# A two-layer cross-attention kernel: the image outputs of the last four heads on GpSimd, the image softmax behind the normalization, one Gram group a step earlier

## The chip, the cores and the metric

One core of a Trainium2 chip runs the kernel. The metric is the device time of one launch in microseconds (us), the median of several runs. The profile is of one execution, with times in us from the start of its span. Engines: PE (matrix multiply; PEld its weight loads), DVE (VectorE), ACT (ScalarE), POOL (GpSimd), SP (the queue that issues the DMAs).

## The reference

Two cross-attention layers, one after the other, over 64 sequences of 256 rows and 320 channels (20 heads of 16), each with its own context of 77 rows of 512 channels. All is float32. Layer 0 is plain attention. Layer 1 adds an image branch:

```
q = heads(x @ W_q);  k_t, v_t from the first 73 context rows;  k_ip, v_ip from the last 4
probs_t  = softmax(q k_t / 4);            text_out = probs_t v_t
qsem     = l2norm(probs_t @ text_ehs);    sem = qsem @ l2norm(ip_ehs)
probs_ip = softmax(q k_ip / 4 + 0.5 sem) * spatial_mask          # 4 tokens per head
out      = (text_out + probs_ip v_ip) @ W_out + b_out + x
```

(Layer 0 has 77 context rows as text, and an image branch is formed only in layer 1.) The change concerns the product `probs_ip v_ip`, for heads 16 to 19, and when the softmax of `probs_ip` is computed.

## The kernel before

**Steps.** Two sequences (b = 0, 1) make a pair p, 32 pairs in all. The attention of a pair in one layer is cut into ten units: for each b, five units u of 128 rows by 8 heads (the fifth holds the last four heads of both row halves). The main loop runs over steps g; p = g // 10 and k = g % 10 name a step ("step 7" is k = 7). Step g computes the scores of layer 0 for unit g, the scores of layer 1 for unit g - 13, and the products with the Gram matrix and the values ("semantics", L755 and L761) of layer 1 for unit g - 15. All three go into one PSUM tile `sc`, which takes four banks and exists once. So the first semantics of a step (L755) can't start until ACT has copied `sums` (L1064) out of the `sc` of the step before, and that copy waits for DVE to have read `sc` for the last time (L772, L775). The start of the first L755 is used below as the start of a step.

**What each engine does in a step, in order.** PE: semantics, scores (L641), the transposes of layer 1's probabilities (L705, L706), a first group of fillers, the transposes of layer 0's probabilities (again L705, L706), a second group of fillers, and after units 1 and 4 the products with the values (`pv`, L788, L793). DVE: what is in `early`, draining a projection (L601) in steps 0 and 2, row maxima and differences of both layers (L659, L661), the products with the Gram result (L772, L775), layer 0's row sums and their reciprocals (L687, L688), what is in `later`, and a last reduction (L1136). ACT: copies of the transposes (L712 layer 1, L731 or L720 layer 0), the exponential of layer 0 (L669), `sums` (L1064), the exponentials of layer 1 (L672, L673), copies for the fillers. POOL: a small copy (L676), the normalization of layer 0's probabilities (L692), and many small products that place values, keys and Gram matrices in block form.

**Fillers.** `fillers(k, p)` is a table written by hand: which keys, queries, values, Gram matrices and projections are made in which step, for pairs p + 1 to p - 3. `add(0, ...)` is the first group, `add(1, ...)` the second, `add(2, ...)` the third, after the second. Each takes one of two PSUM tiles `ms` (pool `pms`) in turn; transposes take one of two tiles `tr` (pool `ptr`) in turn. In 6 of the pairs 2 to 30 (3, 8, 13, 18, 23, 28) steps 6 and 8 hold two groups of `value_rows` (L379), otherwise one.

**The image branch of layer 1.** Five units after its first, a sequence is through (`ends`, in step 4 or 9). Then, by steps: `image_scores` (L882 on DVE, L883 and L884 on POOL) is put in `later` of the next step (5 or 0); `image_shifted` (`most`, L889 on DVE; L890 on POOL) and `image_exponential` (`num`, L893 on ACT) in `early` of the step after (6 or 1); `image_weights` (L900, L901 on DVE; L902, L850 on POOL) in `early` of the third (7 or 2). `later` runs ahead of the normalization, `early` at the head of a step. In step 7 `image_transposed` (L914, `itr`) transposes the weights of both sequences, all 80 columns (20 heads of 4 tokens); in step 8 `image_attend` multiplies heads 0 to 15 with the block-diagonal image values (L926), and `image_attend_last` heads 16 to 19 (L947, 80 rows), which DVE adds to `last` (L951). The block values `vip` are loaded by 20 DMAs per sequence (L475).

**The text branch.** `text_output` (step 4 or 9) divides by the row sums on POOL (L850, `an`); `text_transposed` (steps 5 and 0) transposes two blocks of 128 channels per row half (L837) and the last 64 channels (L838), and ACT copies both (L840, L841) to `main` and `last`, which `project` of layer 1 reads in step 9.

**Order.** `keep_order` fixes the order as written on PE, ACT, DVE and POOL. An instruction that waits holds up all that follow on its engine. The order of SP's DMAs after the first steps is chosen by the framework's scheduler.

## Time and profile before

| | us |
|---|---|
| median of 3 runs (lowest, highest) | 2617.92 (2614.57, 2618.2) |
| profiled execution, device time | 2612.19 |
| its span, first to last instruction | 2610.4 |
| one pair in the middle, ten steps | 77.44 |

The profiled execution is 5.7 us below the median. Its granted TensorE clock is 0.998 over the span. The steps are very regular: the starts of the first L755 of each step, read from the timeline over the whole trace, give these lengths, as medians over the pairs 3 to 30:

| step | 0 | 1 | 2 | 3 | 4 | 5 | 6 | 7 | 8 | 9 |
|---|---|---|---|---|---|---|---|---|---|---|
| us | 8.08 | 9.39 | 8.61 | 7.45 | 8.68 | 6.42 | 6.95 | 6.96 | 7.09 | 7.81 |

In the six pairs with two groups of `value_rows`, step 6 takes 9.10 and step 8 takes 9.24. A line of the timeline view gives start, duration, engine, line, operation, what is written from what, the count of merged instructions, and in brackets the engine's idle time before it with what ended it.

### The profile page before, as it was taken

The numbers are of one execution on the slowest core, as the hardware profiler recorded it, in microseconds if no ns is written. First come the engines' busy times: TensorE is split into PE (matmuls) and PEld (weight loads), VectorE is DVE, ScalarE is ACT, GpSimd is POOL, SyncE is SP. The second block draws the span as 40 slices with busy tenths as digits, with TensorE's granted clock in tenths as the row PEclk, the third lists the DMA queues.
The fourth block names the chain that finished last, engine by engine and source line by source line (L and its number), as shares of the span: only waits on it lengthen the run. The fifth ranks groups of instructions, "written<-read, shape, count | busy, mean of one in ns | idle before, by whom it ended". The sixth has DMA issues, their size and how long they took to land.

```text
span 2610.4 us, 74097 instructions
## 1 busy us (share of the span) xinstructions
PE 2552.0 (98%) x27026; PEld 1979.1 (76%) x27026; DVE 1971.3 (76%) x3641; ACT 1535.6 (59%) x3989; POOL 1439.9 (55%) x3514
## 2 busy tenths in 40 slices
PE   7999999999999999999999999999999999999998
PEld 5677777777777777777777777777777777777677
DVE  4577777777787777787777787777777778777864
ACT  3465665665665665665665665665665566666553
POOL 2456555566555556555556555556555565555542
PEclk9999999999999999999999999999999999999999
DMA  5212211112111112111112111112111112111100
GB/s 164 72 29 58 58 43 48 43 51 55 52 51 38 51 51 55 55 48 39 51 52 55 51 52 43 47 52 56 52 51 39 51 53 55 47 50 34 29 22 23
DMA packets 154658, 132.28 MB, mean 51 GB/s; under 512 B 48248, under 2 KB 132984, under 8 KB 154296
## 3 DMA queue, kind: packets, MB, share of 16 engines
q1 hardware_dynamic: 153432, 126.38, 18.0%
q8 instruction: 217, 3.56, 0.6%
q14 instruction: 145, 1.19, 0.2%
q10 hardware_dynamic: 864, 1.15, 0.1%
HBM read 89.53 MB, written 33.91 MB: 47 GB/s over the span
## 4 chain that ended last, share of the span: by engine, by line
PE 84%; DVE 7%; DMA 3%; ACT 2%; POOL 1%; issue 1%; SPq 1%; DVEq 0%; POOLq 0%; ACTq 0%
PE sc L755 12%; PE tr L705 11%; PE o_ps L528 8%; PE sc L641 7%; PE v_ps L379 6%; PE sc L761 4%; PE q_ps L528 4%; PE q_ps L555 4%; PE k_ps L334 3%; PE o_ps L616 3%; DVE w L661 3%; PE pv L788 2%; PE o_ps L537 2%; DVE mx L659 2%; PE q_ps L557 2%; PE rtr L706 2%
## 5 line engine op out<-in xcount | busy, mean ns | idle before, releaser
L659 DVE TENSOR_REDUCE mx<-sc 128x8 f32<-128x584 f32 (+1 forms) x640 | 497.3, 777 | 446.9 <-PE sc L641 446.8
L692 POOL TENSOR_TENSOR parts<-w,sm 128x512 f32<-128x512 f32 (+1 forms) x640 | 439.5, 707 | 301.9 <-ACT parts L673 177.8
L661 DVE TENSOR_TENSOR w<-sc,mx 128x616 f32<-128x616 f32 x640 | 511.8, 800 | 67.0 <-ACT w L669 0.5
L712 ACT COPY pt<-tr 128x512 f32<-128x512 f32 x320 | 186.8, 584 | 431.9 <-PE tr L705 427.5
L705 PE MATMUL tr<-ident,parts 128*128 128x128 f32 x2560 | 409.6, 283 | 12.5 <-POOL parts L692 5.2
L755 PEld LDWEIGHTS sc<-gv,pt 64*128 64x128 f32 x5120 | 316.9, 187 | 96.0 <-ACT sums L1064 47.3
L705 PEld LDWEIGHTS tr<-ident,parts 128*128 128x128 f32 x2560 | 282.5, 141 | 123.4 <-issue 88.0
L755 PE MATMUL sc<-gv,pt 64*128 64x94 f32 x5120 | 356.3, 278 | 17.4 <-ACT sums L1064 17.2
L676 POOL COPY att<-w 128x32 f32<-128x32 f32 x320 | 66.8, 209 | 469.7 <-DVE w L661 469.2
L669 ACT ACTIVATE w<-w 128x616 f32<-128x616 f32 x320 | 232.0, 725 | 96.7 <-DVE w L661 95.8
L687 DVE TENSOR_REDUCE sm<-w 128x8 f32<-128x616 f32 x320 | 247.9, 775 | 13.6 <-ACT w L669 13.6
L641 PE MATMUL sc<-kbd,q 32*128 32x154 f32 x5120 | 248.2, 306 | 1.0 <-ACT q L586 0.8
L528 PE MATMUL o_ps<-aT,wo 128*128 128x256 f32 x1024 | 231.6, 379 | 0.0
L1136 DVE TENSOR_REDUCE nrm<-prod 128x8 f32<-128x584 f32 x320 | 227.3, 710 | 0.4
L772 DVE TENSOR_TENSOR prod<-sc,parts 128x512 f32<-128x512 f32 x320 | 217.8, 681 | 4.0 <-PE sc L761 4.0
L528 PEld LDWEIGHTS o_ps<-aT,wo 128*128 128x128 f32 x1024 | 189.7, 190 | 23.0
L672 ACT ACTIVATE parts<-w 128x512 f32<-128x512 f32 x320 | 207.1, 647 | 0.0
L641 PEld LDWEIGHTS sc<-kbd,q 32*128 32x128 f32 x5120 | 187.0, 187 | 6.2 <-issue 5.4
L731 ACT COPY pt<-tr 128x512 f32<-128x512 f32 x256 | 151.1, 590 | 67.1 <-PE tr L705 66.8
L379 PE MATMUL v_ps<-wv,cf 128*128 128x320 f32 (+1 forms) x624 | 182.1, 438 | 0.0
L706 PE MATMUL rtr<-ident,parts 128*104 128x128 f32 (+1 forms) x640 | 174.8, 273 | 0.0
L1064 ACT COPY sums<-sc 128x168 f32<-128x168 f32 x320 | 96.4, 301 | 122.5 <-DVE prod L775 121.3
(151 smaller groups left out, 4840.0 us busy)
## 6 DMA issues: line engine op xcount, KB each, us to landing
vip<-vip_rows SPq DMA_DIRECT2D x1280, 5.0 KB
out_dram<-x SPq DMA_DIRECT2D x64, 256.0 KB
x<-in_x_dram SPq DMA_DIRECT2D x31, 512.0 KB
v_rows<-vs SPq DMA_DIRECT2D x38, 320.0 KB
vm<-v_rows SPq DMA_DIRECT2D x152, 80.0 KB
ct<-in_ctx_dram SPq DMA_DIRECT2D x32, 308.0 KB
cf<-in_ctx_dram SPq DMA_DIRECT2D x38, 256.0 KB
g_rest<-gram_rest SPq DMA_DIRECT2D x512, 0.5 KB
```

Of the source, the lines that this page charges most:

```text
L379: nc.tensor.matmul(ps[:n, :C], cfs[i][:, k, :n], wv[l][:, k, :], start=(k == 0), stop=(k == KE - 1))
L528: nc.tensor.matmul(ps[b][:, m, :], w[:, k, m * P : (m + 1) * P], main[:, k, b * S : (b + 1) * S], start=(k == 0 and m == 0), stop=False,)
L641: nc.tensor.matmul(ps[:, r, 2 * T * l : 2 * T * (l + 1)], q[rows, b, :] if part == 2 else q[rows, t0 : t0 + P], kbd[rows, part].rearrange( ...
L659: nc.vector.tensor_reduce(mx, sc[:, :, :, :nt], AX.X, ALU.max)
L661: nc.vector.tensor_tensor(w, sc, mx.unsqueeze(3).broadcast_to([P, 4, 2, T]), ALU.subtract)
L669: nc.scalar.activation(w, w, AF.Exp, scale=SCALE)
L687: nc.vector.tensor_reduce(sm, w, AX.X, ALU.add)
L692: nc.gpsimd.tensor_tensor(two[:, 8 * t0 : 8 * t1].rearrange("p (h t) -> p h t", h=8), w[:, :, t0:t1], sm.unsqueeze(2).broadcast_to([P, 8, ...
L705: nc.tensor.transpose(ps[:, i, :], flat[:, i * P : (i + 1) * P], ident)
L706: nc.tensor.transpose(pr[:n, 0, :], flat[:, 4 * P : 4 * P + n], ident)
L755: nc.tensor.matmul(ps[:, i % 2 * 2 + j, at : at + GV], pt[half_rows, i, :], gv[b][half_rows, part, i, :], start=start and i < 2, stop=False,)
L1136: nc.vector.tensor_reduce(eight(stats[q, b][2], u), prod, AX.X, ALU.add)
```

## The change

Three things are moved or replaced.

1. Heads 16 to 19. The image values of the four heads are loaded once per sequence to all 128 partitions (`last_image_values`, one DMA each, in steps 1 and 5). `last_image_outputs` multiplies them on POOL with the image weights, token by token: 4 products and 4 additions per sequence, 128 elements per partition each, in steps 4 (b = 0) and 7 (b = 1), at the end of what POOL gets there. The results are added into the text outputs of these heads, which `text_output` now keeps in a tile of its own. `last_transposed` transposes both sequences in step 8 with two transposes into an `ms` tile, and ACT copies them to `last`. L838, L841, L947 and L951 are gone; the image weights and values of the remaining branch have 64 rows, 16 DMAs per sequence.
2. `later` runs behind the normalization, and `image_shifted` and `image_exponential` go from `early` to `later` of the same step, that is from the head of steps 6 and 1 to their end. `image_weights` stays in `early` of the next step.
3. The Gram group of b = 1 goes from step 6 to step 5, and the placing of layer 1's values for b = 1 from step 7 to step 8, behind `place_gram` and `keys_by_head`.

```diff
@@ image values
-        n, r0 = H * NIP, (2 * p + b) * NIP
-        vip = vips[p, b] = big.tile([n, C], F32, tag="vip", name=f"vip{p}_{b}", bufs=3)
-        for h in range(H):
-            nc.sync.dma_start(vip[h * NIP : (h + 1) * NIP, :], vip_rows[r0 : r0 + NIP, :])
+        n, r0 = HT * NIP, (2 * p + b) * NIP
+        vip = vips[p, b] = big.tile([n, 2 * P], F32, tag="vip", name=f"vip{p}_{b}", bufs=3)
+        for h in range(HT):
+            nc.sync.dma_start(vip[h * NIP : (h + 1) * NIP, :], vip_rows[r0 : r0 + NIP, : 2 * P])
...
+    def last_image_values(p, b):
+
+        r0 = (2 * p + b) * NIP
+        v = vips[p, b, "last"] = small.tile([P, NIP, HALF], F32, tag="vlast", name=f"vlast{p}_{b}", bufs=1)
+        nc.sync.dma_start(v, vip_rows[r0 : r0 + NIP, 2 * P :].unsqueeze(0).broadcast_to([P, NIP, HALF]))
@@ text_transposed
-            nc.tensor.transpose(ps[: rows.stop, 2, :], t[:, C - rows.stop :], ident)
             t0 = b * S + s * P
             nc.scalar.copy(main[:, :, t0 : t0 + P], ps[:, :2])
-            nc.scalar.copy(last[rows, s * P : (s + 1) * P], ps[rows, 2, :])
+
+    def last_image_outputs(p, b):
+
+        v = vips[p, b, "last"].rearrange("p t (h d) -> p t h d", d=D)
+        w, to = weights[p, b, "last"], lasts[p][:, :, b]
+        part = [P, 2, H - HT, D]
+        for t in range(NIP):
+            prod = small.tile(part, F32, tag="ip_last", name=f"ip_last{p}_{b}{t}", bufs=1)
+            nc.gpsimd.tensor_tensor(
+                prod, v[:, t].unsqueeze(1).broadcast_to(part), w[:, :, :, t].unsqueeze(3).broadcast_to(part), ALU.mult
+            )
+            nc.gpsimd.tensor_add(to, to, prod)
+
+    def last_transposed(p):
+
+        ps = pms.tile([P, 512], F32, tag="ms", name=f"ltr{p}")
+        for s in range(2):
+            nc.tensor.transpose(
+                ps[:, s * P : (s + 1) * P], lasts[p][:, s].rearrange("p b h d -> p (b h d)"), ident
+            )
+        nc.scalar.copy(aTs[1, p][1], ps[:, :S])
@@ fillers
         elif k == 4:
...
+            add(1, p - 2, last_image_outputs, p - 2, 0)
             add(1, p + 1, first_queries, p + 1)
         elif k == 5:
...
             add(0, p + 1, keys, 0, p + 1, 0)
+            add(1, p - 1, gram, p - 1, 1)
             add(2, p - 2, text_transposed, p - 2, 1)
+            add(1, p - 2, last_image_values, p - 2, 1)
         elif k == 6:
...
-            add(1, p - 1, gram, p - 1, 1)
             add(1, p, place_image_keys, p)
         elif k == 7:
...
             add(1, p - 2, lambda: made.update(wT=image_transposed(p - 2)))
-            add(1, p - 1, place_values, 1, p - 1, 1)
+            add(1, p - 2, last_image_outputs, p - 2, 1)
             add(1, p - 1, image_values, p - 1, 0)
         elif k == 8:
...
             add(1, p - 1, image_values, p - 1, 1)
-            add(1, p - 2, image_attend_last, p - 2)
+            add(1, p - 1, place_values, 1, p - 1, 1)
+            add(1, p - 2, last_transposed, p - 2)
@@ main loop
         if now[1]:
             exponential(1, g, *now[1])
+        if now[0]:
+            normalize(g)
         for fn, args in later.pop(g, ()):
             fn(*args)
-        if now[0]:
-            normalize(g)
...
                 later[g + 1] = [(image_scores, (q, b))]
-                early[g + 2] = [(image_shifted, (q, b)), (image_exponential, (q, b))]
+                later[g + 2] = [(image_shifted, (q, b)), (image_exponential, (q, b))]
                 early[g + 3] = [(image_weights, (q, b))]
```

More of the change, by code (lines that the diff above doesn't have):

```diff
@@ L246, in tile_two_cross_attentions @@
         nc.gpsimd.tensor_add(head_mask[:, :n], head_mask[:, :n], head_mask[:, n : 2 * n])
-    ip_mask = blocks("ip_mask", H * NIP, H, NIP)
+    ip_mask = blocks("ip_mask", HT * NIP, HT, NIP)
     half = blocks("half", P, 2, M)
@@ L470, in image_values @@
     def image_values(p, b):
-        n, r0 = H * NIP, (2 * p + b) * NIP
-        vip = vips[p, b] = big.tile([n, C], F32, tag="vip", name=f"vip{p}_{b}", bufs=3)
-        for h in range(H):
-            nc.sync.dma_start(vip[h * NIP : (h + 1) * NIP, :], vip_rows[r0 : r0 + NIP, :])
+        n, r0 = HT * NIP, (2 * p + b) * NIP
+        vip = vips[p, b] = big.tile([n, 2 * P], F32, tag="vip", name=f"vip{p}_{b}", bufs=3)
+        for h in range(HT):
+            nc.sync.dma_start(vip[h * NIP : (h + 1) * NIP, :], vip_rows[r0 : r0 + NIP, : 2 * P])
     def place_image_values(p, b):
-        n, vip = H * NIP, vips[p, b]
+        n, vip = HT * NIP, vips[p, b]
         v = vip.rearrange("p (h d) -> p h d", d=D)
-        nc.gpsimd.tensor_tensor(v, v, ip_mask[:n].unsqueeze(2).broadcast_to([n, H, D]), ALU.mult)
+        nc.gpsimd.tensor_tensor(v, v, ip_mask[:n].unsqueeze(2).broadcast_to([n, HT, D]), ALU.mult)
+    def last_image_values(p, b):
+        r0 = (2 * p + b) * NIP
+        v = vips[p, b, "last"] = small.tile([P, NIP, HALF], F32, tag="vlast", name=f"vlast{p}_{b}", bufs=1)
+        nc.sync.dma_start(v, vip_rows[r0 : r0 + NIP, 2 * P :].unsqueeze(0).broadcast_to([P, NIP, HALF]))
     grams = {}
@@ L814, in attend @@
             nc.scalar.copy(last, ps[:, 1, :])
+    lasts = {}
     def text_output(p, b):
@@ L821, in text_output @@
         nc.vector.reciprocal(rec, sums[:, :, NIP + D])
-        an = big.tile([P, 2, H, D], F32, tag="an", name=f"an{p}_{b}", bufs=1)
-        by_head(an, sums[:, :, NIP : NIP + D], rec)
+        an = big.tile([P, 2, HT, D], F32, tag="an", name=f"an{p}_{b}", bufs=1)
+        if b == 0:
+            lasts[p] = big.tile([P, 2, 2, H - HT, D], F32, tag="an_last", name=f"an_last{p}", bufs=1)
+        by_head(an, lasts[p][:, :, b], sums[:, :, NIP : NIP + D], rec)
         return an
@@ L830, in text_transposed @@
             aTs[1, p] = channels("aT1", f"aT1_{p}", 1)
-        main, last = aTs[1, p]
-        rows = slice(b * HALF, (b + 1) * HALF)
+        main = aTs[1, p][0]
         for s in range(2):
@@ L837, in text_transposed, with by_head @@
                 nc.tensor.transpose(ps[:, i, :], t[:, i * P : (i + 1) * P], ident)
-            nc.tensor.transpose(ps[: rows.stop, 2, :], t[:, C - rows.stop :], ident)
             t0 = b * S + s * P
             nc.scalar.copy(main[:, :, t0 : t0 + P], ps[:, :2])
-            nc.scalar.copy(last[rows, s * P : (s + 1) * P], ps[rows, 2, :])
+    def last_image_outputs(p, b):
[15 more added lines that the diff above has]
+        nc.scalar.copy(aTs[1, p][1], ps[:, :S])
     one = const.tile([P, 1], F32, tag="one", name="one")
-    def by_head(to, t, factor):
+    def by_head(to, last, t, factor):
         n = t.shape[2]
-        for s, h0, at in ((0, 0, 0), (1, HT, H), (1, 0, H + 4)):
-            m = H if s == 0 else H - HT if h0 else HT
-            nc.gpsimd.tensor_tensor(
-                to[:, s, h0 : h0 + m], t[:, at : at + m],
-                factor[:, at : at + m].unsqueeze(2).broadcast_to([P, m, n]), ALU.mult,
-            )
+        for out, at in ((to[:, 0], 0), (last, HT), (to[:, 1], H + 4)):
+            m = H - HT if out is last else HT
+            full = [P, 2, m, n] if out is last else [P, m, n]
+            k = 2 * m if out is last else m
+            x, f = t[:, at : at + k], factor[:, at : at + k]
+            if out is last:
+                x = x.rearrange("p (s h) d -> p s h d", s=2)
+                f = f.rearrange("p (s h) -> p s h", s=2)
+            nc.gpsimd.tensor_tensor(out, x, f.unsqueeze(len(full) - 1).broadcast_to(full), ALU.mult)
     nums = {}
@@ L902, in image_weights @@
         nc.gpsimd.tensor_mul(m, m, smask.unsqueeze(2).broadcast_to([P, 2, H]))
-        to = weights[p, b] = small.tile([P, 2, H, NIP], F32, tag="iw", name=f"iw{p}_{b}", bufs=2)
-        by_head(to, num, r)
+        to = weights[p, b] = small.tile([P, 2, HT, NIP], F32, tag="iw", name=f"iw{p}_{b}", bufs=2)
+        last = weights[p, b, "last"] = small.tile(
+            [P, 2, H - HT, NIP], F32, tag="iw_last", name=f"iw_last{p}_{b}", bufs=1
+        )
+        by_head(to, last, num, r)
     weights = {}
     def image_transposed(p):
-        n = H * NIP
+        n = HT * NIP
         ps = ptr.tile([P, 4, P], F32, tag="tr", name=f"itr{p}")
@@ L941, in image_attend @@
         return [lambda i=i: out_of(i) for i in range(2)]
-    def image_attend_last(p):
-        wT, last = made["wT"], aTs[1, p][1]
-        ps = pms.tile([P, 512], F32, tag="ms", name=f"ipv{p}_2")
-        for b in range(2):
-            nc.tensor.matmul(
-                ps[b * HALF : (b + 1) * HALF, :S], vips[p, b][:, 2 * P :], wT[:, b * S : (b + 1) * S],
-                start=True, stop=True,
-            )
-        nc.vector.tensor_add(last, ps[:, :S], last)
     made = {}
@@ L982, in fillers @@
             add(1, p - 1, project, 0, p - 1)
+            add(1, p - 2, last_image_values, p - 2, 0)
             add(1, p - 1, place_gram, 0)
```

## Prediction

> **What bounds the kernel now.** First the page, busy time and the chain of waits:

> ```profile
> PE 2552.0 (98%) x27026; PEld 1979.1 (76%) x27026; DVE 1971.3 (76%) x3641; ACT 1535.6 (59%) x3989; POOL 1439.9 (55%) x3514
> PE 84%; DVE 7%; DMA 3%; ACT 2%; POOL 1%; issue 1%; SPq 1%; DVEq 0%; POOLq 0%; ACTq 0%
> ```

> PE is busy nearly always and is 84% of the chain, so PE work taken out should pay, unless a step falls to its next limit. That limit is in the timeline, steps 5 to 7 of pair 17 (PE, then ACT):

> ```profile
> 1364.52 1.03 PE L755 MATMUL sc<-gv,pt 64*128 64x94 f32 x16
> ...
> 1370.94 1.13 PE L755 MATMUL sc<-gv,pt 64*128 64x94 f32 x16 [0.32 <-ACT sums L1064]
> ...
> 1370.58 0.30 ACT L1064 COPY sums<-sc 128x168 f32<-128x168 f32 x1 [0.48 <-DVE prod L775]
> ```

> Step 5 lasts 6.42 us, and PE waited 0.32 us of it for `sums`. So a step has a **floor of about 6.4 to 6.5 us**: PE's semantics and scores (2.1 us), then DVE's row from `mx` to `prod`, then `sums`. Other steps are PE-bound, with little to spare above that. Step 7 next (DVE, ACT, PE):

> ```profile
> 1378.52 0.31 DVE L900 TENSOR_REDUCE imx<-num 128x40 f32<-128x160 f32 x1
> 1378.87 0.40 DVE L901 RECIPROCAL imx<-imx 128x40 f32<-128x40 f32 x1
> 1380.05 0.80 DVE L659 TENSOR_REDUCE mx<-sc 128x8 f32<-128x616 f32 x1 [0.78 <-PE sc L641]
> ...
> 1382.63 0.59 ACT L731 COPY pt<-tr 128x512 f32<-128x512 f32 x1
> ...
> 1383.28 0.63 PE L914 MATMUL itr<-ident,iw 128*80 128x128 f32 x4
> ```

> The step starts at 1377.89 and DVE's `mx` 2.16 us into it, right behind PE's scores, because `imx` was done long before. PE's `itr` starts 0.06 us after ACT's L731, which frees its `tr` tile, and L731 stands in ACT's queue behind the exponential L669, which waits for DVE. Two single-line views say how regular this is, the first of L914, the second of L620:

> ```profile
>   ACT pt L731: 7.2, 30
>   PEld q_ps L557: 25.2, 30
> ```

> L914 has waited for L731 in 30 pairs, and L557 for DVE's L620 in 30 pairs: in steps 7 and 2 **PE already follows DVE**. Whoever makes DVE late there stops PE.

> **The softmax behind the normalization.** All times are from the start of step 6, in this pair (1370.94), and everything is in program order on each engine. Now `most` and L890 come early, and L893 waits only for POOL:

> ```profile
> 1373.32 0.47 POOL L890 TENSOR_TENSOR num<-num,most 128x160 f32<-128x160 f32 x1
> ...
> 1373.83 0.34 ACT L893 ACTIVATE num<-num 128x160 f32<-128x160 f32 x1 [0.78 <-POOL num L890]
> ...
> 1378.15 1.37 POOL L692 TENSOR_TENSOR parts<-w,sm 128x512 f32<-128x512 f32 x2 [1.57 <-ACT parts L673]
> ```

> Afterwards L890 stands behind L692, which starts at 7.21 (1378.15) and takes 1.33 until the next can start: L890 8.54 to 9.01, L893 9.05 to 9.39. `image_weights` is still at the head of step 7's DVE queue: `imx` 9.44, its reciprocal 0.35 later, and `mx` can start 0.31 after that (as the next instruction starts after other 128x40 reciprocals), at 10.10. Step 7 will start at 6.50 (below), and `mx` is due 2.16 into it, at 8.66. **DVE is 1.44 us late in step 7.** Behind `imx` are queued `mx`, `w`, `prod`; for these wait ACT's L669, L731, `sums`, and for L731 PE's `itr`. L731 ends 5.33 into step 7 now and 6.77 then; from `itr` to the step's end PE has 1.57 us, so step 7 takes 6.83 + 1.57 = 8.40 instead of 6.96: **+1.44**. Were it only the floor (`sums`), it would be 6.54 + 1.44 + 0.06 = 8.04, +1.08.

> Step 2 has the same with b = 0. Step 1 is long (9.26, below), so L893 ends at 0.12 of step 2, `imx` and its reciprocal follow, and DVE starts draining the projection (L601) at 0.84 instead of 0.20. The four L601 take 1.66, `mx` starts at 2.47 instead of 2.06, L620 is 0.41 later and L557 with it: **+0.41**. In the six pairs with two row groups step 6 lasts 8.47, `mx` isn't late in step 7, and only step 2 pays.

> What goes: in step 1 ACT waited 2.48 us for L890 ahead of the copies of the transposes, and PE's layer 0 transposes came 0.67 us after L570 began, against 0.54 in step 3: **-0.13**. In step 6 that wait hid behind `v_ps`: 0.

> **PE work.** Step 8 loses L947 (1391.35 to the next step at 1391.94: 0.59) and gets two transposes at 0.125 (four L705 take 0.50 to the next): -0.33, to 6.76; `sums` there ends 6.69 in, so that is all there is. Steps 0 and 5 lose two L838 each at 0.11 (1370.01 to 1370.12): -0.22 each. The Gram group is 0.63 (1377.26 to 1377.89). Step 5 has 6.42 - 0.32 = 6.10 of PE work, and gets 6.10 - 0.22 + 0.63 = 6.51: **+0.09**, its stall filled. Step 6 has 6.95 - 0.63 = 6.32, below the floor: `sums` ends 6.44 in, so 6.50: **-0.45** (in the six pairs the full -0.63). L951 on DVE (0.42) and ACT's L841 (four of 0.27 a pair) go where these engines are not late: nothing.

> **POOL.** A product and an addition of 128 elements aren't in the trace. Nearest: 128x64 at 0.30, 128x104 at 0.37 to 0.40, 128x154 at 0.44, 128x160 at 0.49 to 0.52. I take 0.41 and 0.45 with 0.08 between dependent ones (L883 to L884): 3.8 us for the eight, between 2.8 (0.35 each) and 4.8 (0.52 plus the gap).

> [...]

> In step 4 the eight run from 1.7 to 5.5 of step 5, until its L676 is due (5.36): free. In step 7 the normalization ends 1.7 into step 8, the eight at 5.5; `last_transposed` comes at 6.4, with 0.9 to spare. L938 (2.36) follows to 7.8, 1.1 into step 9, and the projection that reads it starts 2.6 in. Then L676, L692, the Gram placing (1.24), keys (1.14) and the moved `place_values` (3.48): POOL is done 0.6 into step 0. L761 reads the last of it 1.06 into step 0: free, by 0.4 us. But `least` (L866) is queued behind, DVE's drain of the projection in step 0 starts 0.7 later, and Gram and `pv` there wait about 0.15: step 0 is -0.22 + 0.15 = **-0.07**. With 4.8 us for the eight it is about 1 us more.

> **DMA.** SP issues a `vip` load in 0.36 us (20 in 7.28), eight fewer per pair; two loads to 128 partitions come in. The b = 0 one stands in SP's order behind `kl` and must wait until POOL has read the tile (5.5 into step 8), with `vip`, `v_rows` and `vm` loads behind it. These then land about 0.6 into step 0; L480 on POOL needs them past 4 there. Nothing; without that cover POOL waits and step 0 grows. The context load, which waited up to 18.9 us for the Gram group, comes earlier.

> **The sum.** Usual pair, steps 0, 1, 2, 5, 6, 7, 8: -0.07 - 0.13 + 0.41 + 0.09 - 0.45 + 1.44 - 0.33 = **+0.96**; pairs 2 to 30 hold 23: +22.1. The six others: -0.07 - 0.13 + 0.41 + 0.09 - 0.63 - 0.33 = -0.66, in all -4.0. The first pair -0.5; pair 31's steps (2 and 7 as above, no gain in 5, 6, 8): +1.6. At the end POOL is in the chain: L883 at 2589.48 waits for nothing but DVE, and will stand behind the eight of step 4, which begin when L850 ends (2588.66): +3 less 0.5 of PE work, +2.5. Sum: +21.7. On the profiled execution's 2612.19 that is 2633.9. This execution is the lowest of four; their mean (2612.19, 2614.57, 2617.92, 2618.2) is 2615.7, and I forecast from that: **2637 us**, +0.7% on the median.

> **Rivals.**
> - *The gain shows* (faster): the exponent is ready in time, DVE never late. Steps 7 and 2 then add nothing: 23 x -0.89 + 6 x -1.07 - 0.5 - 0.2 + 2.5 = -25, 2591 us. It decides if L893 ends by 7.95 of step 6 instead of 9.39 (0.66 of `imx` work ahead of 8.66). For it: PE is 98% busy. Against: L692 alone ends past 8.5.
> - *POOL is the bound*: the eight take 4.8 us or SP's blocked queue brings loads late, and step 0 stalls by 1 us more in each usual pair: +23 on the forecast, 2660 us, or more.
> - *They cancel* (within 0.2%, which is about what a measurement of this kernel can tell from no change): DVE's lateness is half absorbed, step 7 costs about 0.7: 2620 us.

> **Chances.** Forecast 0.63; POOL 0.15; cancel 0.09; gain 0.13. The forecast's own range is 2625 to 2650; the range 2612 to 2668 leaves out the gain and the worst of POOL. Of cancel I put 0.08 within 0.2% and 0.01 faster: faster 0.14, same 0.08, slower 0.78.

> **What would show it.** Right: in step 7 DVE idles ahead of `imx` until ACT's `num`, step 7 is about 8.4 us, step 6 about 6.5, step 8 about 6.8. Wrong: `mx` of step 7 at 2.16 into the step. POOL rival: step 0 longer than 8.08, PE waiting for POOL at its head. The forecast fails most easily if step 6 does not fall to its floor (then step 7 gains what step 6 keeps), or on POOL's durations.

## The result and the profile after

The changed kernel takes **2630.84 us** (median of 6 runs, 2628.36 to 2634.62) against 2615.02 (6 runs, 2613.88 to 2618.2): ratio 1.0059, 95% interval 1.0046 to 1.0072. It is slower by 15.8 us; 2637 were forecast. The profiled execution took 2628.88, its span 2627.2, against 2612.19 and 2610.4 before.

Lines of kernel.py have moved: L692, L890, L893, L900, L914 (`itr`), L557 and L620 of the kernel before are L699, L922, L925, L932, L949, L564 and L627 here. The page of the changed kernel, busy times and the chain that ended last:

```profile
PE 2541.4 (97%) x26834; PEld 1973.4 (75%) x26834; DVE 1951.9 (74%) x3609; ACT 1521.1 (58%) x3893; POOL 1651.4 (63%) x4026
PE 61%; DVE 15%; POOL 6%; DMA 5%; ACT 5%; SPq 4%; issue 3%; DVEq 0%; POOLq 0%; ACTq 0%
```

PE has 10.6 us less to do and the kernel is slower. PE's share of the chain went from 84% to 61%, DVE's from 7% to 15%, POOL's from 1% to 6%: the chain now passes through POOL, ACT and DVE to PE. The timeline of the changed kernel shows where, in pair 17 (step 6 starts at 1373.82, step 7 at 1380.41, step 8 at 1388.68):

```profile
1381.14 1.38 POOL L699 TENSOR_TENSOR parts<-w,sm 128x512 f32<-128x512 f32 x2 [1.58 <-DVE most L921]
1382.47 0.47 POOL L922 TENSOR_TENSOR num<-num,most 128x160 f32<-128x160 f32 x1
...
1382.98 0.34 ACT L925 ACTIVATE num<-num 128x160 f32<-128x160 f32 x1 [1.93 <-POOL num L922]
...
1383.35 0.32 DVE L932 TENSOR_REDUCE imx<-num 128x40 f32<-128x160 f32 x1 [1.53 <-ACT num L925]
1383.70 0.40 DVE L933 RECIPROCAL imx<-imx 128x40 f32<-128x40 f32 x1
1384.02 0.74 DVE L666 TENSOR_REDUCE mx<-sc 128x8 f32<-128x616 f32 x1
...
1386.47 0.59 ACT L738 COPY pt<-tr 128x512 f32<-128x512 f32 x1
...
1387.09 0.68 DVE L779 TENSOR_TENSOR prod<-sc,parts 128x512 f32<-128x512 f32 x1
1387.12 0.63 PE L949 MATMUL itr<-ident,iw 128*64 128x128 f32 x4 [1.21 <-ACT pt L738]
1388.68 1.13 PE L762 MATMUL sc<-gv,pt 64*128 64x94 f32 x16
```

Read it downwards: the normalization (L699) holds POOL until 1382.47, then come `num`, its exponential, `imx`, and only then `mx`, 3.61 us into step 7 (2.16 before). PE stands idle for 1.21 us ahead of `itr`, and step 7 lasts 8.27 us. The waits view of the changed kernel (total us, times, longest) and the view of L949 say how often:

```profile
DVE imx L932 <- ACT num L925: 92.8, 64, 1.5
...
PEld q_ps L564 <- DVE x L627: 31.9, 30, 1.4
```

```profile
  ACT pt L738: 65.3, 48
```

DVE waits for `num` in all 64 sequences. The view of L949 adds the waits of PE's matmuls and of its weight loads. By the waits view, the matmuls waited 29.9 us ahead of `itr` in 24 places, and 1.0 us in one place before; the weight loads 35.4 us in 24 places, and 6.2 in 29 before. (So the 7.2 us in 30 places, read ahead of the prediction, were weight loads but for one.) The weight loads at L564 in step 2 wait 31.9 us instead of 25.2.

### The profile page after: what moved, and what is told of

Same layout as the page of the kernel before. It is cut to its first block, busy times and chain, and to the rows that moved or that the text cites. A ratio compares the mean times of both kernels' runs of the same rounds, so it can differ in the third digit from the quotient of the medians.

```text
span 2627.2 us, 73845 instructions
## 1 busy us (share of the span) xinstructions
PE 2541.4 (97%) x26834; PEld 1973.4 (75%) x26834; DVE 1951.9 (74%) x3609; ACT 1521.1 (58%) x3893; POOL 1651.4 (63%) x4026
## 3 DMA queue, kind: packets, MB, share of 16 engines
q8 instruction: 215, 3.52, 0.6%
q10 hardware_dynamic: 864, 1.15, 0.1%
## 4 chain that ended last, share of the span: by engine, by line
PE 61%; DVE 15%; POOL 6%; DMA 5%; ACT 5%; SPq 4%; issue 3%; DVEq 0%; POOLq 0%; ACTq 0%
PE sc L762 9%; PE tr L712 7%; PE sc L648 5%; DVE w L668 5%; PE q_ps L535 4%; PE v_ps L379 4%; PE o_ps L535 4%; DVE mx L666 3%; PE sc L768 3%; PE k_ps L334 3%; PE pv L795 3%; POOL parts L699 3%; PE q_ps L564 2%; DVE prod L779 2%; PE pv L800 2%
## 5 line engine op out<-in xcount | busy, mean ns | idle before, releaser
L699 POOL TENSOR_TENSOR parts<-w,sm 128x512 f32<-128x512 f32 (+1 forms) x640 | 439.6, 708 | 401.8 <-DVE sm L695 165.2
L676 ACT ACTIVATE w<-w 128x616 f32<-128x616 f32 x320 | 231.0, 722 | 163.0 <-DVE w L668 155.3
```

The source lines that it names most:

```text
L676: nc.scalar.activation(w, w, AF.Exp, scale=SCALE)
L699: nc.gpsimd.tensor_tensor(two[:, 8 * t0 : 8 * t1].rearrange("p (h t) -> p h t", h=8), w[:, :, t0:t1], sm.unsqueeze(2).broadcast_to([P, 8, ...
```

## The experiments

**Theory.** The late image exponential (part 2) costs the time in steps 7 and 2; the other two parts gain, as the terms of the sum say. **Rivals**: the work on POOL (part 1) is what costs; or the parts can't be added up, since one hides what another costs. All step lengths, medians over the 23 usual pairs of 2 to 30 (those with one group of `value_rows` in steps 6 and 8; first semantics to first semantics), in us; "31" is pair 31, "end" the time from the start of pair 33:

| kernel | time | 0 | 1 | 2 | 5 | 6 | 7 | 8 | 9 | 31 | end |
|---|---|---|---|---|---|---|---|---|---|---|---|
| before | 2615.0 | 8.08 | 9.39 | 8.61 | 6.42 | 6.95 | 6.96 | 7.09 | 7.81 | 74.6 | 47.4 |
| after | 2630.8 | 7.98 | 9.29 | 8.85 | 6.42 | 6.59 | 8.26 | 6.75 | 7.81 | 81.2 | 52.1 |
| e1, without part 2 | 2609.9 | 8.03 | 10.19 | 8.61 | 6.42 | 6.49 | 6.95 | 6.75 | 7.82 | 79.4 | 53.7 |
| e2, part 2 alone | 2643.4 | 8.08 | 9.29 | 8.80 | 6.41 | 6.95 | 7.90 | 7.09 | 7.82 | 85.9 | 47.4 |
| e3, Gram alone | 2603.8 | 8.08 | 9.40 | 8.61 | 6.56 | 6.49 | 6.96 | 7.09 | 7.82 | 77.2 | 47.4 |
| e4, heads alone | 2624.8 | 8.01 | 10.19 | 8.61 | 6.42 | 6.95 | 6.95 | 6.75 | 7.82 | 76.9 | 53.5 |
| e5, softmax by sequence | 2591.4 | 8.01 | 9.29 | 8.54 | 6.42 | 6.49 | 6.95 | 6.75 | 7.81 | 78.0 | 53.4 |
| e6, e5 and the end | 2584.8 | 8.00 | 9.29 | 8.54 | 6.41 | 6.49 | 6.95 | 6.75 | 7.81 | 78.0 | 47.2 |
| e7, e1 and values back | 2703.5 | 7.86 | 9.61 | 8.61 | 6.42 | 6.49 | 6.95 | 9.64 | 9.38 | 85.1 | 53.4 |

Steps 3 and 4 are left out (their medians are 7.45, and 8.68 to 8.69, everywhere). The steps, pair 31 and the end are read from one profiled execution of each kernel. The time is a median of several runs, for e7 of one run.

**e1: the changed kernel without part 2.**

```diff
@@ main loop of the changed kernel
-        if now[0]:
-            normalize(g)
         for fn, args in later.pop(g, ()):
             fn(*args)
+        if now[0]:
+            normalize(g)
...
-                later[g + 2] = [(image_shifted, (q, b)), (image_exponential, (q, b))]
+                early[g + 2] = [(image_shifted, (q, b)), (image_exponential, (q, b))]
```

> The changed kernel with its second part undone: image scores ahead of the normalization, shift and exponent at the head of steps 6 and 1 as in the kernel before. The heads on POOL, the two transposes, the Gram group in step 5 stay. My theory (image_weights at the head of the next step's DVE queue waits for the late exponent, and PE follows DVE): step 7 back from 8.26 to about 6.96, step 2 from 8.85 to 8.61, step 1 back to 9.39, while step 6 stays near 6.6, step 8 near 6.75, step 0 near 7.98; per usual pair about -0.8 against the kernel before, and with the end's +4.8 about 2594 us. Rival (the added POOL and DMA work is what costs, the order of the softmax is of no account): 2625 to 2631 us, step 7 stays above 8.

Measured 2609.85, ratio 0.9985 (0.9976 to 0.9994). Steps 7 and 2 are back at 6.95 and 8.61: the theory holds there. But the total is 16 us above the expected 2594, and the main place is step 1: 10.19 instead of 9.39. The timeline of e1, pair 17, whose step 1 starts at 1324.95:

```profile
1317.63 0.27 POOL L898 TENSOR_TENSOR least<-sums 128x40 f32<-128x40 f32 x1
...
1324.59 0.49 POOL L915 TENSOR_TENSOR num<-sums,nrm 128x160 f32<-128x160 f32 x1 [1.25 <-DVE nrm L914]
...
1325.64 1.38 POOL L699 TENSOR_TENSOR parts<-w,sm 128x512 f32<-128x512 f32 x2
...
1327.65 0.62 POOL L459 TENSOR_TENSOR vr<-vr,rest 104x256 f32<-104x256 f32 x1
...
1328.59 0.47 POOL L922 TENSOR_TENSOR num<-num,most 128x160 f32<-128x160 f32 x1
...
1329.10 0.34 ACT L925 ACTIVATE num<-num 128x160 f32<-128x160 f32 x1 [3.18 <-POOL num L922]
...
1330.05 0.63 PE L712 MATMUL tr<-ident,parts 128*128 128x128 f32 x4 [0.86 <-ACT pt L719]
```

Step 0 starts at 1316.93 here and at 1322.31 in the kernel before, whose `least` is this line:

```profile
1322.25 0.27 POOL L866 TENSOR_TENSOR least<-sums 128x40 f32<-128x40 f32 x1 [3.52 <-ACT sums L1064]
```

Before, POOL had 3.52 us to spare ahead of `least`. Now it works without such a pause from the eight (the products and additions of the last four heads, 1304.05 to 1308.03) to the last of `place_values` (1317.56), and `least` comes 0.70 us into step 0 instead of 0.06 ahead of it. As an estimate from these rows: 3.97 us of the eight, plus 0.34 by which step 8 is shorter, less 3.52, make 0.79 of lateness; it is 0.76. The lateness goes on from there: DVE waits for `least`, L915 on POOL waits 1.25 us for DVE's `nrm`, and the normalization, queued behind L915, starts 0.69 us into step 1 (1325.64), where before it started about 0.1 us ahead of it. L922 follows 3.64 into the step (2.85 before), ACT's exponential waits 3.18 us for it, and the copies of the transposes stand behind that exponential. PE waits 0.86.

**e2, e3, e4: each part alone in the kernel before.** e2 is the edit of part 2, e3 moves one line (the Gram group), e4 is the edit of part 1 with `place_values` in step 8:

```diff
@@ e3, fillers of the kernel before: k == 5 gains, k == 6 loses
+            add(1, p - 1, gram, p - 1, 1)
...
-            add(1, p - 1, gram, p - 1, 1)
```

> The kernel before with the second part alone: later behind the normalization, shift and exponent in later instead of early. My theory: step 6 stays 6.95, DVE's mx in step 7 comes at about 10.1 - 6.95 = 3.15 us into the step instead of 2.16, step 7 gains about 1.0, step 2 about 0.25, step 1 loses 0.1: about +26 us, 2641 us. Rival (POOL and DMA work costs): no change, 2615 us.

> The kernel before with the Gram group of b = 1 in step 5 instead of step 6, nothing else. My theory: step 5 gets 6.10 + 0.55 to 0.63 of PE work, so 6.65 to 6.75 instead of 6.42; step 6 falls from 6.95 to about 6.5 (floor); -0.1 to -0.2 per usual pair, -0.3 in the six with two row groups: 2608 to 2612 us. Rival (a step's length is PE work alone, no floor): nothing gained beyond the stall of 0.32, which would be -0.32 per pair, 2605 us.

> The kernel before with the last four heads on POOL, the two transposes in step 8 and place_values in step 8; Gram group in step 6 and softmax order as before. My theory: step 8 -0.34, step 0 -0.1, step 5 nothing (it is at its floor of 6.42), and the end +4.8: about -13 + 5 = -8 us, 2607 us. Rival (POOL load costs): 2620 us or more, with PE or DVE waiting for POOL in steps 8, 9 or 0.

- e2: 2643.36, ratio 1.0109 (1.0094 to 1.0125). Part 2 alone costs more than the whole change, in step 7 (+0.94; its step 6 keeps PE's 6.95, so less lateness is left over) and step 2 (+0.19).
- e3: 2603.82, 0.9964 (0.9951 to 0.9976). Step 6 falls to 6.49, the floor; step 5 rises by 0.14 only. The total is below the theory's 2608 to 2612 and next to the rival's 2605, but not for the rival's reason: with PE work alone, step 6 would have fallen to 6.95 - 0.63 = 6.32.
- e4: 2624.84, 1.0044 (1.0031 to 1.0056). The theory's 2607 is wrong. Step 8 gains 0.34 and step 0 0.07, but step 1 shows the same 10.19 as e1, and the end is 6 us longer.

Together e2 to e4 make +29.0 - 10.5 + 10.5 = 29.0 us on the median of before in their set (2614.34), yet the change costs 15.8: **the parts can't be added**. Pair 31 and the end, where the clock differs (below), are not the reason: in the profiles, pairs 2 to 30 alone give +22.8 - 9.8 + 3.3 = +16.3, against +5.5 for the change. Behind the normalization, L922 no longer holds up ACT in step 1. That takes away the 0.80 us that part 1 puts there (10.19 becomes 9.29). So part 2, added to the two others, gains 0.9 us in step 1 and costs 0.24 in step 2 for b = 0, and costs 1.3 in step 7 for b = 1.

The step 5 of e3 shows what PE really had free there. Timeline of e3, pair 17, step 5 from 1358.27 to 1364.83:

```profile
1362.28 0.27 PE L706 MATMUL rtr<-ident,parts 128*104 128x128 f32 x1
1362.39 0.70 PE L493 MATMUL g_ps<-ct 128*73 128x77 f32 x8
1363.02 0.64 PE L788 MATMUL pv<-pt,v 128*32 128x256 f32 x8
...
1364.63 0.27 PE L838 MATMUL atr<-ident,an 128*128 128x128 f32 x1
1364.83 1.13 PE L755 MATMUL sc<-gv,pt 64*128 64x94 f32 x16
```

The same places in the kernel before:

```profile
1368.53 0.27 PE L706 MATMUL rtr<-ident,parts 128*104 128x128 f32 x1
1368.73 0.64 PE L788 MATMUL pv<-pt,v 128*32 128x256 f32 x8
...
1370.34 0.27 PE L838 MATMUL atr<-ident,an 128*128 128x128 f32 x1
```

From L706 to `pv` it is now 0.74 us, where it was 0.20 before (1368.53 to 1368.73): the Gram group adds 0.54, not 0.63. And after the last L838 the next step starts 0.20 later here, against 0.60 before (1370.34 to 1370.94): the stall was 0.40, not the 0.32 in the brackets, which count from the end that the list gives L838, 0.27 after its start, where in e3 the next matmul starts 0.20 after it. 6.42 + 0.54 - 0.40 = 6.56, as measured.

**e5: each sequence where it pays.** The changed kernel with b = 1 as before the change (scores ahead of the normalization, exponential at the head of step 6, by a queue `ahead`), and b = 0 wholly behind the normalization, its `image_weights` too:

```diff
+        for fn, args in ahead.pop(g, ()):
+            fn(*args)
         if now[0]:
             normalize(g)
...
-                later[g + 1] = [(image_scores, (q, b))]
-                later[g + 2] = [(image_shifted, (q, b)), (image_exponential, (q, b))]
-                early[g + 3] = [(image_weights, (q, b))]
+                (ahead if b else later)[g + 1] = [(image_scores, (q, b))]
+                (early if b else later)[g + 2] = [(image_shifted, (q, b)), (image_exponential, (q, b))]
+                (early if b else later)[g + 3] = [(image_weights, (q, b))]
```

> The changed kernel with the order of the image softmax chosen per sequence: b = 1 as in the kernel before (scores ahead of the normalization in step 5, shift and exponent at the head of step 6, weights at the head of step 7), b = 0 behind the normalization throughout, its weights too (end of step 2 instead of its head). My theory, now with two terms (the late exponent makes DVE late in the next step; and with the heads on POOL an early exponent of b = 0 waits behind POOL's place_values and holds ACT's copies in step 1, +0.8): step 1 stays 9.29, step 2 is back at 8.61, step 6 about 6.5, step 7 about 6.95, steps 0 and 8 as changed; about -1.0 per usual pair against before, about 2588 us. Rival (what costs is POOL's and the DMAs' load as such): 2605 us or more.

Measured 2591.41, ratio 0.9910 (0.9895 to 0.9925): the theory, corrected by e1 to e4, holds to 3.4 us, and it holds in the steps: 9.29 in step 1, 8.54 in step 2, 6.95 in step 7. The timeline of e5, pair 17, step 7 (from 1361.01):

```profile
1362.11 0.31 DVE L932 TENSOR_REDUCE imx<-num 128x40 f32<-128x160 f32 x1
...
1363.17 0.80 DVE L666 TENSOR_REDUCE mx<-sc 128x8 f32<-128x616 f32 x1 [0.32 <-PE sc L648]
```

`imx` waits for nothing, and `mx` starts 2.16 us into the step, right behind PE's scores.

**e6: the end.** At the end of the kernel POOL is in the chain, as the timeline of the changed kernel shows:

```profile
2600.53 0.41 POOL L858 TENSOR_TENSOR ip_last<-vlast,iw_last 128x128 f32<-128x128 f32 x1
2601.02 0.46 POOL L861 TENSOR_TENSOR an_last<-an_last,ip_last 128x128 f32<-128x128 f32 x1
...
2604.51 0.49 POOL L915 TENSOR_TENSOR num<-sums,nrm 128x160 f32<-128x160 f32 x1
...
2605.64 0.32 DVE L921 TENSOR_REDUCE most<-num 128x40 f32<-128x160 f32 x1 [4.33 <-POOL num L916]
...
2608.42 0.87 PE L949 MATMUL itr<-ident,iw 128*64 128x128 f32 x2 [3.30 <-POOL iw L885]
```

L915 stands behind the eight of b = 0, which hold POOL for 3.98 us and could run earlier: POOL is idle for 8.20 us ahead of `least` at 2597.89. e6 runs them a step earlier in the last pair:

```diff
@@ fillers, in k == 3
+            if p - 2 == NP - 1:
+                add(1, p - 2, last_image_outputs, p - 2, 0)
@@ in k == 4
-            add(1, p - 2, last_image_outputs, p - 2, 0)
+            if p - 2 < NP - 1:
+                add(1, p - 2, last_image_outputs, p - 2, 0)
```

> The run before this one, and in the last pair alone the eight products and additions of b = 0 one step earlier (step 3 instead of 4), where POOL has nothing to do. My theory (at the end these eight stand in the chain ahead of the image scores): the stretch after the last pair's first step falls by about 3.9 us, to 48 to 49 us; 2584 us. Rival (the end is bound by PE or by the text outputs): no change against the run before.

Measured 2584.77, ratio 0.9886 (0.9869 to 0.9902). The end falls from 53.44 to 47.22 us, 0.2 below that of before. That is more than the 3.9 us expected; in the profile of e5 the granted clock is 0.50 for 10.24 us within this stretch, in that of e6 only in the last 1.0 us of the span, so part of the fall may be the clock. Timeline of e6: the last of the eight is done at 2557.64, and L915 follows its own releaser:

```profile
2557.18 0.46 POOL L861 TENSOR_TENSOR an_last<-an_last,ip_last 128x128 f32<-128x128 f32 x1
...
2563.03 0.49 POOL L915 TENSOR_TENSOR num<-sums,nrm 128x160 f32<-128x160 f32 x1 [0.81 <-DVE nrm L914]
```

**This version beats both kernels**: the one before by 1.1%, the changed one by 1.75% of its median.

**e7: is it `place_values` that makes step 1 late?** e1, with that one line back in step 7:

```diff
@@ fillers of e1: k == 7 gains ahead of last_image_outputs, k == 8 loses
+            add(1, p - 1, place_values, 1, p - 1, 1)
...
-            add(1, p - 1, place_values, 1, p - 1, 1)
```

> The kernel of the first run of the first set (softmax order as before) with place_values of b = 1 back in step 7, ahead of the eight. My theory (step 1's +0.8 there comes from POOL being busy with place_values into step 0, which makes least, DVE's drain and POOL's shift late): step 1 returns from 10.19 to 9.39 to 9.5; in exchange POOL's addition to main ends about 4 us into step 9, after the projection that needs it is due (2.6), so step 9 grows by 1.0 to 1.7. Rival (step 1's +0.8 comes from the eight or the DMAs as such): step 1 stays 10.2.

Step 1 falls from 10.19 to 9.61, as the theory has it, but the time is 2703.52 us (one run), with 9.64 in step 8 and 9.38 in step 9. The timeline of e7, pair 17, end of step 8, and POOL ahead of the next step 0 (1444.35):

```profile
1436.17 0.44 PE L867 MATMUL ltr<-ident,an_last 128*128 128x128 f32 x2 [2.69 <-POOL an_last L861]
1436.54 1.13 PE L762 MATMUL sc<-gv,pt 64*128 64x94 f32 x16
...
1444.28 0.27 POOL L898 TENSOR_TENSOR least<-sums 128x40 f32<-128x40 f32 x1 [2.13 <-ACT sums L1093]
```

Now `last_transposed` waits for POOL's eight, and PE, in order, with it. This also means that e7 does not answer its question. Step 8 is 2.89 us longer than in e1, and POOL has that time too: `least`, 0.76 us late in e1, now comes when it is due and finds that POOL has been idle for 2.13 us, and 0.76 + 2.13 = 2.89. So the stall of PE accounts for all of POOL's earliness, and the place of `place_values` for none that these rows show. The rival (the eight as such) is not refuted; the estimate under e1 speaks for it, but no run has the eight in time without `place_values` behind them. The 0.22 us that step 1 keeps above 9.39 are what step 0 gained (7.86 instead of 8.08): DVE and POOL run there as before, PE is earlier. Of the two orders, that of the changed kernel (the eight in step 7, `place_values` behind) is the better one, and what POOL's lateness costs in step 1 has to be hidden in another way, as e5 does.

Step 9 was expected to grow because the projection would wait for POOL. It didn't: it takes 7.81 us in the 13 pairs of 2 to 30 in which the clock (next paragraph) stays, and 9.37 or more in the 16 in which it falls near the start of the step. So of the 89 us over the median of before, part is the clock.

**e8 and e9: the clock in pair 31.** In pair 31 steps 5 and 7 of the changed kernel take 10.56 and 8.98 us, against 6.79 and 6.77 before. The windows view (length; PE, PEld, DVE, ACT, POOL busy; granted clock; DMA) of the changed kernel around the start of step 5 (2468.12), then of the kernel before around the same place (2462.07):

```profile
2464.93:2468.34 3.41, 1.15 (x13) 0.90 (x11) 3.28 (x6) 2.23 (x7) 0.72 (x3) 1.00 0.13 34
2468.34:2471.75 3.41, 3.41 (x41) 2.93 (x40) 1.75 (x5) 3.35 (x6) 3.04 (x7) 0.50 0.00 0
2471.75:2475.17 3.42, 2.87 (x15) 2.49 (x15) 3.18 (x5) 1.31 (x4) 2.95 (x8) 0.50 0.00 0
...
```

```profile
2457.63:2461.05 3.42, 2.18 (x18) 1.93 (x18) 3.17 (x5) 2.29 (x6) 1.77 (x4) 1.00 0.21 55
2461.05:2464.46 3.41, 2.39 (x43) 2.14 (x44) 3.22 (x8) 2.70 (x6) 1.99 (x5) 1.00 0.00 0
2464.46:2467.87 3.41, 1.88 (x25) 1.10 (x23) 3.24 (x5) 2.76 (x7) 1.59 (x4) 1.00 0.00 0
```

Both kernels leave PE idle for 2.26 us ahead of this step. In the changed one the idle time lies within one stretch of 3.41 us, with PE busy for 1.15 of it, and the clock is 0.50 in the next three (two are shown). In the kernel before it is split over two stretches with 2.18 and 2.39 us of PE work, and the clock stays. e8 is e6 with work for PE in the idle times (transposes of the identity that nobody reads), e9 is e6 once more:

```diff
@@ main loop of e6, behind the layer 0 transposes
+        if idle in (-6, -4):
+            keep_busy(14 if idle == -6 else 8)
```

> e6 with 14 transposes of the identity, read by nobody, on PE behind pair 31's step 4, and 8 behind its step 6 (1.75 and 1.0 us at full clock), where PE is idle for 2.26 and 1.31 us. Theory (PE's idle time brings the lower clock): the granted clock keeps at 1.00 through pair 31, step 5 of that pair falls from 10.5 us to 6.8 or less, the pair from 78.0 to about 74.5, and the kernel by about 3.5 us against the same kernel without the transposes, run beside it: about 2581. Rival (the drop hangs on something else, the stage's low DMA traffic or the load of the other engines): the clock falls to 0.5 there as before, step 5 stays above 10, and the time is the same within 1 us or rises a little.

> The kernel of e6 once more, for e8 to be compared with on the same chip. Theory: 2584 to 2586, pair 31's step 5 at 10.5 us with the clock at 0.5 in it, as in e6, if the drop belongs to the kernel. Rival (the drop is chance): step 5 at 6.8 in this profiled execution, pair 31 at 74.

e8 took 2586.34 (0.9892, 0.9875 to 0.9910), e9 2583.37 (0.9879, 0.9864 to 0.9894). With the added work the clock stayed at 1.00 in step 5, but the gain did not come. Windows view of e8:

```profile
...
2436.41:2439.83 3.42, 3.42 (x48) 2.59 (x46) 3.25 (x8) 2.81 (x10) 2.95 (x9) 1.00 0.00 0
2439.83:2443.24 3.41, 1.83 (x33) 1.34 (x31) 2.78 (x5) 0.73 (x3) 3.09 (x8) 1.00 0.19 43
2443.24:2446.65 3.41, 2.21 (x9) 1.81 (x10) 3.27 (x8) 2.93 (x9) 0.77 (x2) 0.50 0.03 6
```

With PE kept busy (2.45 us in the stretch ahead of step 5, 2429.59 to 2433.00, against 1.15 in the changed kernel) the clock stays through step 5, which takes 6.65 us (9.13 in e9, 10.49 in e6). That speaks against the rival that the drop hangs on something else; it is one profiled execution each. But step 5 being short, PE idles for 2.32 us in step 6, behind `num` on POOL and ACT, and the clock falls there: 10.72 us instead of 6.49. The drop has moved by one step, pair 31 takes 79.1 (76.6 in e9), and no gain is left.

## Why the prediction was nearly right, step by step

The direction, the mechanism and the steps were right, the total is 6 us off, and two errors of opposite sign hide in it.

| usual pair, step | 0 | 1 | 2 | 5 | 6 | 7 | 8 | sum |
|---|---|---|---|---|---|---|---|---|
| predicted | -0.07 | -0.13 | +0.41 | +0.09 | -0.45 | +1.44 | -0.33 | +0.96 |
| measured | -0.10 | -0.10 | +0.24 | 0.00 | -0.36 | +1.30 | -0.34 | +0.64 |

- **Step 7**: `mx` was foreseen 3.60 us into the step and came at 3.61 (the normalization started 0.11 later than foreseen and step 6 lasted 0.09 longer, which cancel). What was mis-sized is DVE's row behind it. From `mx` to `prod` it took 3.22 us before (1380.05 to 1383.27) and takes 3.07 now (1384.02 to 1387.09): `mx`, which now follows the reciprocal without a pause, is listed with 0.74 instead of 0.80, and `w` starts 0.77 behind it instead of 0.90. Whether the missing pause is the reason is open: in step 0 of the kernel before, `mx` follows L601 without a pause and is listed with 0.80. So 1.30 and not 1.44.
- **Step 2**: the same 0.11 (3.22 to 3.11), and `mx` was 0.35 late instead of 0.41: +0.24.
- **Step 5**: 0.40 of stall and 0.54 of Gram group instead of 0.32 and 0.63 (e3). With the two L838 gone, PE's work is 6.34, below the floor, which stays at 6.42.
- **Step 6** fell to 6.59, not 6.50; e1, e3 and e5 all show 6.49. From `mx` to `prod` DVE takes 3.23 us in it and 3.13 in e5, where `most` runs just ahead; whether that is the reason wasn't tried.
- **Steps 0, 1, 8** agree within 0.03. Step 1 agrees for a reason that the prediction did not see: it took POOL's delay into account for step 0 (`least`) and not for L890 in step 1. Without part 2 that delay costs 0.80 us there (e1, e4). So the working credited part 2 with 0.13 in step 1, and it is worth 0.90 in this kernel. This also sinks the rival "the gain shows" as it was priced: 2591 us needs not only the exponent in time for b = 1, but also b = 0 left behind the normalization. e5, which does both, measured 2591.41. That the two numbers agree is luck: e5's profile is 31.0 us shorter than that of before in pairs 2 to 30 (the rival had 26.9) and 9.4 longer in pair 31 and the end (the rival had 2.3).
- **Pairs 2 to 30**: predicted +18.1, measured +5.5. The usual pairs gave 23 x 0.51 (means; the kernel before has extra time of 0.4 to 1.2 us in step 4 of four pairs, the changed one 1.5 us in one) = +11.7, the six others 6 x -1.06 = -6.4 instead of -4.0.
- **Pair 31**: predicted +1.6, measured +6.6. Steps 5, 7 and 8, with the clock at 0.50 for 10.24 and 3.41 us, hold 3.77 + 2.21 + 0.64 of it, and only 1.44 was foreseen, in step 7. This term failed: the sum had nothing for the clock.
- **The end**: predicted +2.5, measured +4.7. The eight take 3.98 us, 0.82 of which L915 would have waited for DVE anyway (before, L850 ends at 2588.66 and L883 starts at 2589.48), so about 3.2, less 0.5, where 3 less 0.5 was foreseen. That leaves 2.0; in this stretch the clock is at 0.50 for 6.83 us, behind the 3.30 us in which PE waits for `iw`, and the sum had nothing for that. No run separates the two.
- **The rest**: up to pair 2 +0.7 (predicted -0.5), pair 32 -0.8 (not in the sum).
- **POOL's operations**: 0.41 and 0.45 to 0.46, the eight 4.0 us, against 3.8 (2.8 to 4.8). The rival that POOL makes step 0 longer is out: step 0 is shorter than before.

So about 12 us too much in the middle stand against some 7 us too little behind it.

## What to carry to other kernels

Where engines work in order, follow a late instruction through everything queued behind it until something was due: here `mx`, 1.45 us late in step 7, made the step 1.30 us longer, with PE 97% busy over the span and 10.6 us of its work gone. Put the same operation of two interleaved streams in different places if their surroundings differ: behind the normalization was right for one sequence (0.9 us gained in step 1, 0.24 lost in step 2) and wrong for the other (1.3 us lost). Parts of a change share queues, so a part measured alone says little of its worth beside the others; the version that keeps what each place needs came out only after all three had been taken apart. And an experiment that stalls one engine gives the others time: what then runs earlier there (e7) need not do so because of the edit.
